# Attention over time and bands, then a feed-forward: the softmax weights become the stationary operand of the weighing, with a constant column beside the values

## The chip, the core and the metric

The kernel runs on one core of one Trainium2 chip. The time is device time in microseconds (us) of one execution of the whole program. The engines are TensorE (PE; its weight loads are listed apart as PEld), VectorE (DVE), ScalarE (ACT), GpSimd (POOL) and SyncE (SP), which issues most DMAs. Smaller is better.

## The reference

The input x has shape (2, 256, 128, 128): batch, time T, band FB, channel C. Three residual steps follow one another: causal attention along time, attention along bands within 16 bands of the query, and a feed-forward with 512 hidden channels. Everything is float32.

```python
def _mha(x, wi, bi, wo, bo, h, mask):
    qkv = x @ wi.T + bi
    q, k, v = jnp.split(qkv, 3, axis=-1)          # 4 heads of 32 channels
    scores = jnp.einsum('...hqd,...hkd->...hqk', q, k) * (1.0 / np.sqrt(dh)) + mask
    attn = jax.nn.softmax(scores, axis=-1)
    o = jnp.einsum('...hqk,...hkd->...hqd', attn, v)
    return o.swapaxes(-2, -3).reshape(x.shape) @ wo.T + bo

xt = _ln(x, ln_t_w, ln_t_b).transpose(0, 2, 1, 3)
x = x + _mha(xt, t_wi, t_bi, t_wo, t_bo, H_T, cm).transpose(0, 2, 1, 3)   # cm: causal, 256 steps
xf = _ln(x, ln_f_w, ln_f_b)
x = x + _mha(xf, f_wi, f_bi, f_wo, f_bo, H_F, bm)                          # bm: |i - j| <= 16
xn = _ln(x, ln_n_w, ln_n_b)
x = x + (gelu(xn @ w1.T + b1, approximate=False) @ w2.T + b2)
```

## The kernel before

A test on the device of how large the scores can become (`fold`) chooses between two paths; with these inputs the program takes `BoundedPath`, in which the exponential needs no row maximum. The other path isn't touched.

**Groups.** The work is cut into groups of 512 tokens: four tiles of 128 tokens. There are 128 groups of attention over time (`OverTime`: two bands of 256 steps each), 128 of attention over bands (`OverBands`: four time steps of 128 bands each) and 128 of feed-forward (`FeedForward`). All time groups come first; then eight band groups and the eight feed-forward groups that use them alternate. `run` is a software pipeline written out by hand: iteration n does one stage of each of several neighbouring groups, and every engine executes in exactly the order in which `run` emits (the wrapper `InOrder`). This is also why nearly all instructions in the profile carry the one line L924: it is the wrapper's.

**One attention group, stage by stage.** `normalize` and `turn` make the layer norm on DVE and transpose it in 32x32 blocks on DVE (the tile z), DMAs through DRAM (turned) finish the transpose, and `fetch` brings it back as xnT: channels on partitions, 512 tokens along the row. `queries_keys` and `values` multiply by the folded weights wf, and ACT copies the results out of PSUM as qT, kT and v. The scores go into PSUM with the keys on partitions and the queries along the row; ACT takes the exponential (tiles p; pf over bands), and POOL zeroes what the mask forbids. Over time the weights are in two tiles: p0 has the first 128 keys against all 256 queries, p1 the last 128 keys against the last 128 queries.

**Column tiles.** A product with 128 output rows is issued as four matmuls with 32 stationary columns each, one for each 32-column strip of the array, writing 32 partitions of PSUM each (`product`, `rows_of`). Such a matmul appears in the profile as "128*32" (rows * columns of the array). A float32 matmul of the program shows as two matmuls and two loads in the profile.

**The weighing (`weigh`, L758 over time, L845 over bands).** The stationary operand is v of one head (32 columns), and the softmax weights stream past as the moving operand, 128 to 256 queries at a time; the result op has channels on partitions and tokens along the row. A second set of matmuls with a stationary block of ones sums the weights into rp, in the same layout, each sum repeated on 32 partitions. Over time POOL first adds p1 to the part of p0 that belongs to the same queries (`add`, two calls), so that one pass of ones suffices.

**The division.** `invert` takes the logarithm of rp and the exponential of its negative on ACT (ln, then r). `divide` refines this by one Newton step on DVE (two operations, the second making u, with its sign reversed), and a third DVE operation multiplies op by u into oT. The reversed sign is taken up by wn, which is the output weight times -1. At the 16 places where band groups give way to feed-forward groups (`turn` in `run`), `invert_exactly` uses DVE's reciprocal instead, so that ACT needn't change its table.

**The output.** `output` multiplies oT by wn one iteration later, and `finish` adds the result to the residual on DVE.

**PSUM.** There are eight banks of 128x512. Over time their use is a fixed rotation (`banks`, `place`); over bands they are taken in turn (`turn_of_bank`).

**Order.** Iteration n over time emits for PE: scores of groups n and n+1, the output projection of group n-2, the weighing of n-1, queries and keys and then values of n+2. Over bands: scores of n, weighing of n-1, output projection of n-2, queries, keys and values of n+1. DVE's queue holds in each iteration the layer-norm work of groups three to eight ahead, the residual of n-2 and the division of n-1.

Of the kernel before, what the change touches and what calls it, by code (L numbers as in the profile page):

```python
# [19 lines left out]
P = 128  # L20
H = 4
# [10 lines left out]
BANK = 512  # L32
HALF = P // 2
LARGE = 1e20
EXP_SET = "natural_log_exp_and_others"


# [382 lines left out]
    return t.rearrange("p (t i q) -> p i t q", i=NT, q=D)  # L420


def by_tile(t):

    return t.rearrange("p (i t q) -> p i t q", i=NT, q=D)


class Group:
# [126 lines left out]
    def take_values(self):  # L555
        pass
# [1 line left out]
    def weigh(self):  # L558
        pass

    def invert(self):
        pass

    def divide(self):
        pass

# [25 lines left out]
class Attention(Group):  # L592
# [33 lines left out]
            product(path, self.vp[:, i], self.xnT[:, i * P : (i + 1) * P], wv, turn=2 if i in self.swapped else 0)  # L626

    def take_values(self):
        path = self.path
        self.v = path.work.tile([P, NT, P], F32, name="v", bufs=4)  # L630
        path.scalar.copy(self.v, self.vp)

    def invert(self):

        path = self.path
        ln = path.work.tile([P, NT * P], F32, name="ln", bufs=2)
        path.scalar.activation(ln, self.rp, AF.Ln)
        self.r0 = path.work.tile([P, NT * P], F32, name="r0", bufs=2)
        path.scalar.activation(self.r0, ln, AF.Exp, scale=-1.0)

    def invert_exactly(self):
        self.r0 = None
        self.r = self.path.work.tile([P, NT * P], F32, name="ln", bufs=2)
        self.path.vector.reciprocal(self.r, self.rp)

    def divide(self):

        path, vector = self.path, self.path.vector
        if self.r0 is None:
            self.oT = path.work.tile([P, NT * P], F32, name="oT", bufs=2)  # L650
            u = path.work.tile([P, NT * P], F32, name="u", bufs=2)
            vector.tensor_tensor(by_rows(u), by_tile(self.op), by_tile(self.r), ALU.mult)
            vector.tensor_scalar(self.oT, u, -1.0, None, ALU.mult)
            return
        vector.tensor_tensor(self.rp, self.rp, self.r0, ALU.mult)
        u = path.work.tile([P, NT * P], F32, name="u", bufs=2)
        vector.scalar_tensor_tensor(u, self.rp, 2.0, self.r0, ALU.subtract, ALU.mult)
        self.oT = path.work.tile([P, NT * P], F32, name="oT", bufs=2)
        vector.tensor_tensor(by_rows(self.oT), by_tile(self.op), by_tile(u), ALU.mult)

    def output(self):
        path = self.path
# [21 lines left out]
class OverTime(Attention):  # L684
# [15 lines left out]

    def take_values(self):
        path = self.path
        self.v = path.work.tile([P, NT, P], F32, name="v", bufs=4)
        for s in range(2):
            path.scalar.copy(self.v[:, 2 * s : 2 * s + 2], self.vp[s])

    def first_tiles(self):
        path = self.path
# [4 lines left out]
    def second_tiles(self):  # L713
        path = self.path

        self.p1 = path.work.tile([P, 2, H, 2, P], F32, name="p1", tag="h", bufs=2)
        self.s1 = {h: path.bank([P, 2, P], "sp", path.banks[f"b{h}"]) for h in range(H)}

    def first_scores(self, h, s, e):
# [16 lines left out]

    def second_weights(self, heads):
        for h in heads:
            self.path.scalar.activation(self.p1[:, :, h, 0], self.s1[h], AF.Exp)

    def mask(self, blk, base=0):
        path = self.path
# [6 lines left out]
        self.mask(self.p0[:, :, :, 0:P])  # L749

    def mask_second(self):
        self.mask(self.p1[0:HALF, :, :, 0], -HALF)
        self.mask(self.p1[HALF:P, :, :, 0, 0:HALF])

    def add(self, s):
        self.path.gpsimd.tensor_tensor(self.p1[:, s, :, 1], self.p1[:, s, :, 0], self.p0[:, s, :, P : 2 * P], ALU.add)

    def weigh(self):  # L758
        path, v = self.path, self.v
        rp = path.bank([P, 2, 2, P], "rp", self.place.get("rp"))  # L760
        for n in range(2):
            for h in range(H):
                w = self.p1[:, :, h, 1] if n else self.p0[:, :, h, 0:P]
                path.tensor.matmul(rp[rows_of(h), :, n], path.k.ones[:, 0:D], w, start=True, stop=True)
        op = path.bank([P, 2, 2 * P], "op", self.place.get("op"))
        for s in range(2):
            for h in range(H):
                r = rows_of(h)
                path.tensor.matmul(op[r, s, :], v[:, 2 * s, r], self.p0[:, s, h], start=True, stop=False)
            for h in range(H):  # L770
                r = rows_of(h)
                path.tensor.matmul(
                    op[r, s, P : 2 * P], v[:, 2 * s + 1, r], self.p1[:, s, h, 0], start=False, stop=True
                )
        self.op = op.rearrange("p s q -> p (s q)")
        self.rp = rp.rearrange("p s n q -> p (s n q)")


TIME_ORDER = """
# [19 lines left out]
class OverBands(Attention):  # L799
# [41 lines left out]
    def first_half(self):  # L841
        self.p = self.path.work.tile([P, H, NT, P], F32, name="pf", tag="p", bufs=3)
        self.scores(range(H))

    def weigh(self):  # L845
        path = self.path

        path.held = {name: path.turn_of_bank() for name in self.follow}
        self.rp = path.bank([P, NT * P], "rp")
        for h in range(H):  # L850
            path.tensor.matmul(
                self.rp[rows_of(h), :], path.k.ones[:, 0:D], self.p[:, h].rearrange("p i q -> p (i q)"),
                start=True, stop=True,
            )
        self.op = path.bank([P, NT * P], "op")
        for i in range(NT):
            c = slice(i * P, (i + 1) * P)
            for h in range(H):
                r = rows_of(h)
                path.tensor.matmul(self.op[r, c], self.v[:, i, r], self.p[:, h, i, :], start=True, stop=True)  # L860


class FeedForward(Group):
# [65 lines left out]
class BoundedPath:  # L929
    def __init__(self, ctx, tc, k):  # L930
        self.tc, self.nc, self.k = tc, tc.nc, k
        self.xpool = ctx.enter_context(tc.tile_pool(name="xpool", bufs=3))
        self.work = ctx.enter_context(tc.tile_pool(name="work", bufs=3))
        self.small = ctx.enter_context(tc.tile_pool(name="small", bufs=6))
        ps = ctx.enter_context(tc.tile_pool(name="ps", bufs=1, space=PSUM))
        self.ps = [ps.tile([P, BANK], F32, name=f"bank{i}", tag=f"bank{i}") for i in range(8)]
        self.next_bank = 0
        self.inputs = 0
        self.held = {}
        self.banks = dict(zip(("a1", "a2", "b0", "b3", "a0", "a3", "b1", "b2"), range(8)))  # L940
        self.tensor, self.vector = InOrder(tc, tc.nc.tensor), InOrder(tc, tc.nc.vector)
        self.scalar, self.gpsimd = InOrder(tc, tc.nc.scalar), InOrder(tc, tc.nc.gpsimd)
        self.sync = InOrder(tc, tc.nc.sync)
        self.dram = ctx.enter_context(tc.tile_pool(name="turns", bufs=3, space=DRAM))
        self.zero = 0.0
        self.once = once = ctx.enter_context(tc.tile_pool(name="once", bufs=1))
        self.eps = once.tile([P, 1], F32, name="eps")
        tc.nc.vector.memset(self.eps, EPS)

        self.band = once.tile([P, P], F32, name="band")  # L950
        tc.nc.gpsimd.memset(self.band, 0.0)
        for s in (1, -1):
            tc.nc.gpsimd.affine_select(
                out=self.band, in_=self.band, compare_op=ALU.is_ge, fill=-1e30, base=BAND,
                pattern=[[-s, P]], channel_multiplier=s,
            )

    def turn_of_bank(self):
        i, self.next_bank = self.next_bank, (self.next_bank + 1) % 8
# [109 lines left out]
    def fold_rest(self):  # L1069
# [32 lines left out]
    def warm(self):  # L1102


        for _ in range(8):
            bank = self.bank([P, 3 * P], "warm")
            self.tensor.matmul(bank, self.k.ones, self.k.wf[0], start=True, stop=True)

    def run(self, x, out):
        groups = list(self.groups(x, out))  # L1110
# [24 lines left out]
        for n in range(-12, len(groups) + 2):  # L1135
# [168 lines left out]
```

## Time and profile before

| | |
|---|---|
| median of 3 runs | 2663.48 us (2662.64 to 2663.9) |
| the profiled execution | 2662.95 us |
| its span in the trace | 2661.2 us |
| clock granted to TensorE | 0.999 |
| instructions in the trace | 156426 |
| DMA | 347.08 MB, mean 130 GB/s |

The groups of instructions that the change touches, from the groups by form (busy us is the time in which at least one of the group ran; matmuls on different column tiles run at once):

| engine, operation | shape | count | busy us | mean ns of one |
|---|---|---|---|---|
| PE sums over time, p with ones | 128x256 | 2048 | 134.0 | 379 |
| PE weighted values over time, p with v | 128x256 and 128x128 | 2048 and 2048 | 157.5 and 103.2 | 379 and 273 |
| PE sums over bands, pf with ones | 128x512 | 1024 | 140.6 | 603 |
| PE weighted values over bands, pf with v | 128x128 | 4096 | 140.7 | 273 |
| ACT ln and r | 128x512 | 240 each | 145.5 and 151.3 | 606 and 630 |
| DVE Newton step and product with op | 128x512 | 240 each of three | 166.9, 166.0, 166.0 | 695, 692, 692 |
| POOL adds of p | 128x512 | 256 | 323.9 | 1287 |

The span is cut into 40 slices on the page. The time groups fill roughly the first 14 of them, up to about 935 us; the rest alternates between bands and feed-forward. In a row of the timeline, the first number is the start and the second the time from the first start to the last end of the instructions merged in it.

### The profile page before, as it was taken

Reading aid. Unit: us, or ns where it says so; the run is one execution under the profiler, and the core shown is the slowest. Engines: PE = TensorE matmul, PEld = TensorE weight load, DVE = VectorE, ACT = ScalarE, POOL = GpSimd, SP = SyncE. Lnnn points to the kernel's source line nnn. Section 1 sums busy time; section 2 is a strip of 40 time slices with the busy share of each in tenths; the row PEclk is TensorE's granted clock in tenths of the full one; section 3 lists DMA queues with packets and bytes.
Section 4 is the critical chain, followed back from the end, with each engine's and each line's share of the span. In section 5 each row is a group of like instructions: output and inputs, shape, how many; then the busy total and the mean of one; then the engine's idle time right before and its main releaser. Section 6 shows DMA issues by size and latency. Waiting matters only on the chain.

```text
span 2661.2 us, 156426 instructions
## 1 busy us (share of the span) xinstructions
PE 2630.1 (99%) x68662; PEld 1930.4 (73%) x68662; DVE 2140.1 (80%) x6429; ACT 1841.8 (69%) x3562; POOL 1947.3 (73%) x2297
## 2 busy tenths in 40 slices
PE   7999999999999999999999999999999999999998
PEld 5667667666676668778777687777777877777777
DVE  6988888888888897977868779678687796886874
ACT  6898999989989874664755746647557466475573
POOL 4999999999999986756667667666676676666762
PEclk9999999999999999999999999999999999999999
DMA  6655555555556454444444444444444454544533
GB/s 147 159 155 149 152 153 153 150 151 157 149 154 153 121 129 120 124 122 126 118 118 126 122 118 126 120 125 118 123 125 119 117 129 113 133 118 121 127 95 82
DMA packets 471510, 347.08 MB, mean 130 GB/s; under 512 B 43296, under 2 KB 405152, under 8 KB 470816
## 3 DMA queue, kind: packets, MB, share of 16 engines
q1 hardware_dynamic: 469568, 335.92, 49.0%
q8 instruction: 540, 8.85, 1.5%
q10 hardware_dynamic: 1248, 1.05, 0.2%
q14 instruction: 154, 1.26, 0.2%
HBM read 169.03 MB, written 167.77 MB: 127 GB/s over the span
## 4 chain that ended last, share of the span: by engine, by line
PE 86%; DVE 10%; DMA 2%; SPq 0%; issue 0%; ACT 0%; DVEq 0%; ACTq 0%
PE bank L924 86%; DVE xh L924 2%; DVE bank L924 2%; DVE z L924 1%; DVE u L924 1%; DVE oT L924 1%; DVE stats L924 1%; DVE x L924 1%; DMA xnT<-turned 1%; DMA turned<-z 1%; SPq L924 0%; DVE mv L924 0%; DMA x<-in_x 0%; DMA rows_sb<-in_rows 0%; ACT p L924 0%
## 5 line engine op out<-in xcount | busy, mean ns | idle before, releaser
L924 ACT ACTIVATE hT<-bank,b 128x512 f32<-128x512 f32 x512 | 346.9, 688 | 527.0 <-PE bank L924 496.3
L924 POOL TENSOR_SCALAR_AFFINE_SELECT pf<-pf 128x512 f32<-128x512 f32 x768 | 476.8, 635 | 178.5 <-ACT pf L924 152.2
L924 PEld LDWEIGHTS bank<-w2T_sb,hT 128*32 128x32 f32 x16384 | 498.2, 110 | 22.9 <-issue 16.7
L924 PE MATMUL bank<-xnT,w1f 128*32 128x512 f32 x4096 | 510.0, 592 | 0.0
L924 PE MATMUL bank<-w2T_sb,hT 128*32 128x128 f32 x16384 | 504.0, 273 | 0.2 <-ACT hT L924 0.2
L924 PE MATMUL bank<-xnT,wf 128*32 128x512 f32 x4096 | 492.5, 592 | 3.5 <-ACT p L924 3.0
L924 ACT ACTIVATE p<-bank 128x512 f32<-128x512 f32 (+1 forms) x1024 | 430.4, 495 | 65.0 <-PE bank L924 64.6
L924 POOL TENSOR_SCALAR_AFFINE_SELECT p<-p 128x1024 f32<-128x1024 f32 (+2 forms) x384 | 363.6, 947 | 81.2 <-ACT p L924 72.9
L924 DVE TENSOR_SCALAR xh<-x,mv,rstd 128x160 f32<-128x160 f32 x1040 | 404.4, 431 | 9.7
L924 PEld LDWEIGHTS bank<-wf,xnT 128*32 128x32 f32 x8192 | 243.6, 110 | 144.0 <-issue 103.2
L924 DVE TENSOR_TENSOR res<-bank,res 128x512 f32<-128x512 f32 x256 | 170.5, 666 | 218.8 <-PE bank L924 192.0
L924 PEld LDWEIGHTS bank<-xnT,w1f 128*32 128x32 f32 x4096 | 247.2, 110 | 128.2 <-issue 114.9
L924 POOL TENSOR_TENSOR p<-p,p 128x512 f32<-128x512 f32 x256 | 323.9, 1287 | 10.7
L924 DVE BATCH_NORM_STATS2 stats<-x 128x6 f32<-128x128 f32 x1536 | 329.5, 277 | 0.2 <-DMA x<-in_x 0.2
L924 POOL TENSOR_SCALAR rstd<-mv 128x4 f32<-128x4 f32 x248 | 56.3, 227 | 369.1 <-DVE mv L924 368.3
L924 PE MATMUL bank<-qT,kT 32*64 32x80 f32 (+4 forms) x16384 | 314.3, 273 | 2.4 <-ACT p L924 1.0
L924 PEld LDWEIGHTS bank<-qT,kT 32*64 32x64 f32 x16384 | 271.3, 131 | 54.5 <-ACT kT L924 50.3
L924 ACT ACTIVATE pf<-bank 128x512 f32<-128x512 f32 x512 | 266.7, 602 | 46.7 <-PE bank L924 44.1
L924 PE MATMUL bank<-wn,oT 128*32 128x128 f32 x8192 | 283.4, 274 | 0.7 <-DVE oT L924 0.7
L924 DVE STREAM_TRANSPOSE z<-xh 128x512 f32<-128x512 f32 x384 | 273.3, 712 | 13.2
L924 PE MATMUL bank<-wf,xnT 128*32 128x128 f32 x8192 | 276.7, 273 | 0.0
L924 POOL TENSOR_TENSOR rstd<-rstd,mhalf 128x4 f32<-128x4 f32 x248 | 256.6, 1035 | 20.7
(102 smaller groups left out, 3806.0 us busy)
## 6 DMA issues: line engine op xcount, KB each, us to landing
turned<-z SPq DMA_DIRECT2D x1536, 64.0 KB, 2.7
xnT<-turned SPq DMA_DIRECT2D x384, 256.0 KB, 3.1
x<-in_x SPq DMA_DIRECT2D x128, 256.0 KB, 4.4
x<-res SPq DMA_DIRECT2D x256, 128.0 KB, 2.6
x<-x SPq DMA_DIRECT2D x128, 256.0 KB, 4.2
out<-res SPq DMA_DIRECT2D x256, 128.0 KB, 2.5
w1T_sb<-in_w1T ACTq DMA_DIRECT2D x1, 256.0 KB, 5.7
w2T_sb<-in_w2T ACTq DMA_DIRECT2D x1, 256.0 KB, 7.0
```

The lines of the kernel that those rows point to most:

```text
L924: return self.tc.keep_in_program_order(emit(*args, **kwargs))
```

## The change

The two operands of the weighing swap places. For each head, each 128-token tile and each block t of 32 queries, the 32 columns of softmax weights that belong to these queries are loaded as the stationary operand, and the head's values stream past: 32 channels and a 33rd column that holds a constant (UNIT, 2 to the power -10). The result has the queries on partitions, and beside the 32 weighted values stands the sum of the weights times UNIT. `terms` names which key tiles contribute: one, or two for the later 128 queries over time, which are accumulated in PSUM. So the passes with ones, the adds on POOL, the logarithm and exponential on ACT, the Newton step and the exact reciprocal at the turns are gone. `divide` does for each half (one bank) a DVE reciprocal of 8 sums per partition and a product of 256 values with them, broadcast over the channels, and then one transpose in 32x32 blocks into oT, with channels on partitions again. wn takes up UNIT.

The values live in four fixed tiles (`all_values`) whose constant column is set once by POOL; `next_values` hands them out in turn, and ACT's copy of v skips every 33rd column. p1 loses the room for POOL's sums. The warm-up matmuls at the start, eight in the program, read w1T (512 columns) instead of wf (384).

```diff
+UNIT = 2.0**-10
...
+def by_head(t):
+    return t.rearrange("p i (h d) -> p i h d", h=H)
...
     def take_values(self):
-        path = self.path
-        self.v = path.work.tile([P, NT, P], F32, name="v", bufs=4)
-        path.scalar.copy(self.v, self.vp)
-
-    def invert(self):
...
-    def invert_exactly(self):
...
+        self.v = self.path.next_values()
+        self.path.scalar.copy(self.v[:, :, :, 0:D], by_head(self.vp))
+
+    def weigh(self):
+        path = self.path
+        self.banks = [path.bank([P, 2 * NT, D + 1], name, self.place.get(name)) for name in ("rp", "op")]
+        for half, bank in enumerate(self.banks):
+            for t in range(NT):
+                for i in range(2):
+                    blk = bank[:, 2 * t + i]
+                    terms = self.terms(2 * half + i, t)
+                    for j, (keys, weights) in enumerate(terms):
+                        for h in range(H):
+                            path.tensor.matmul(
+                                blk[rows_of(h)], weights(h), self.v[:, keys, h],
+                                start=j == 0, stop=j == len(terms) - 1,
+                            )
 
     def divide(self):
 
         path, vector = self.path, self.path.vector
...
-        vector.tensor_tensor(self.rp, self.rp, self.r0, ALU.mult)
-        u = path.work.tile([P, NT * P], F32, name="u", bufs=2)
-        vector.scalar_tensor_tensor(u, self.rp, 2.0, self.r0, ALU.subtract, ALU.mult)
+        o = path.work.tile([P, NT, NT, D], F32, name="o", bufs=2)
+        for half, bank in enumerate(self.banks):
+            r = path.small.tile([P, 2 * NT], F32, name="r")
+            vector.reciprocal(r, bank[:, :, D])
+            vector.tensor_tensor(
+                o[:, :, 2 * half : 2 * half + 2].rearrange("p t i d -> p t (i d)"),
+                bank[:, :, 0:D].rearrange("p (t i) d -> p t i d", i=2), r.rearrange("p (t i) -> p t i", i=2).unsqueeze(3).to_broadcast([P, NT, 2, D]), ALU.mult,
+            )
         self.oT = path.work.tile([P, NT * P], F32, name="oT", bufs=2)
-        vector.tensor_tensor(by_rows(self.oT), by_tile(self.op), by_tile(u), ALU.mult)
+        vector.transpose(self.oT, o.rearrange("p t i d -> p (t i d)"))
...
 class OverTime(Attention):
...
+    def terms(self, i, t):
+        s, q = i // 2, slice(i % 2 * P + t * D, i % 2 * P + (t + 1) * D)
+        terms = [(2 * s, lambda h: self.p0[:, s, h, q])]
+        if i % 2:
+            terms.append((i, lambda h: self.p1[:, s, h, t * D : (t + 1) * D]))
+        return terms
...
-        self.p1 = path.work.tile([P, 2, H, 2, P], F32, name="p1", tag="h", bufs=2)
+        self.p1 = path.work.tile([P, 2, H, P], F32, name="p1", tag="h", bufs=2)
...
-    def add(self, s):
-        self.path.gpsimd.tensor_tensor(self.p1[:, s, :, 1], self.p1[:, s, :, 0], self.p0[:, s, :, P : 2 * P], ALU.add)
-
-    def weigh(self):
...
 class OverBands(Attention):
...
+    def terms(self, i, t):
+        return [(i, lambda h: self.p[:, h, i, t * D : (t + 1) * D])]
+
     def weigh(self):
-        path = self.path
-        path.held = {name: path.turn_of_bank() for name in self.follow}
-        self.rp = path.bank([P, NT * P], "rp")
...
+        self.path.held = {name: self.path.turn_of_bank() for name in self.follow}
+        super().weigh()
...
+        self.all_values = [once.tile([P, NT, H, D + 1], F32, name=f"v{i}") for i in range(4)]
+        for v in self.all_values:
+            tc.nc.gpsimd.memset(v[:, :, :, D], UNIT)
...
-            scalar.mul(wn, k.woT[a], -1.0)
+            scalar.mul(wn, k.woT[a], UNIT)
...
-            bank = self.bank([P, 3 * P], "warm")
-            self.tensor.matmul(bank, self.k.ones, self.k.wf[0], start=True, stop=True)
+            bank = self.bank([P, self.k.NI * P], "warm")
+            self.tensor.matmul(bank, self.k.ones, self.k.w1T, start=True, stop=True)
...
-                old.add(0)
-                old.add(1)
...
-            do(n - 1, "invert_exactly" if turn else "invert")
```

More of the change, by code (lines that the diff above doesn't have):

```diff
@@ L559, in weigh @@
         pass
-    def invert(self):
-        pass
     def divide(self):
@@ L628, in take_values @@
     def take_values(self):
+        self.v = self.path.next_values()
+        self.path.scalar.copy(self.v[:, :, :, 0:D], by_head(self.vp))
+    def weigh(self):
         path = self.path
-        self.v = path.work.tile([P, NT, P], F32, name="v", bufs=4)
-        path.scalar.copy(self.v, self.vp)
-    def invert(self):
-        path = self.path
[L636 to L639, printed above, removed]
@@ L641, in invert_exactly @@
-    def invert_exactly(self):
-        self.r0 = None
-        self.r = self.path.work.tile([P, NT * P], F32, name="ln", bufs=2)
-        self.path.vector.reciprocal(self.r, self.rp)
+        self.banks = [path.bank([P, 2 * NT, D + 1], name, self.place.get(name)) for name in ("rp", "op")]
[10 more added lines that the diff above has]
+                            )
@@ L646, in divide @@
     def divide(self):
         path, vector = self.path, self.path.vector
-        if self.r0 is None:
-            self.oT = path.work.tile([P, NT * P], F32, name="oT", bufs=2)
-            u = path.work.tile([P, NT * P], F32, name="u", bufs=2)
-            vector.tensor_tensor(by_rows(u), by_tile(self.op), by_tile(self.r), ALU.mult)
-            vector.tensor_scalar(self.oT, u, -1.0, None, ALU.mult)
-            return
-        vector.tensor_tensor(self.rp, self.rp, self.r0, ALU.mult)
-        u = path.work.tile([P, NT * P], F32, name="u", bufs=2)
@@ L702, in take_values @@
         path = self.path
-        self.v = path.work.tile([P, NT, P], F32, name="v", bufs=4)
+        self.v = path.next_values()
         for s in range(2):
-            path.scalar.copy(self.v[:, 2 * s : 2 * s + 2], self.vp[s])
+            path.scalar.copy(self.v[:, 2 * s : 2 * s + 2, :, 0:D], by_head(self.vp[s]))
+    def terms(self, i, t):
[4 more added lines that the diff above has]
+        return terms
     def first_tiles(self):
@@ L738, in second_weights @@
         for h in heads:
-            self.path.scalar.activation(self.p1[:, :, h, 0], self.s1[h], AF.Exp)
+            self.path.scalar.activation(self.p1[:, :, h], self.s1[h], AF.Exp)
     def mask(self, blk, base=0):
@@ L751, in mask_second @@
     def mask_second(self):
-        self.mask(self.p1[0:HALF, :, :, 0], -HALF)
-        self.mask(self.p1[HALF:P, :, :, 0, 0:HALF])
-    def add(self, s):
-        self.path.gpsimd.tensor_tensor(self.p1[:, s, :, 1], self.p1[:, s, :, 0], self.p0[:, s, :, P : 2 * P], ALU.add)
-    def weigh(self):
[L759 to L776, printed above, removed]
+        self.mask(self.p1[0:HALF], -HALF)
+        self.mask(self.p1[HALF:P, :, :, 0:HALF])
 TIME_ORDER = """
@@ L843, in first_half @@
         self.scores(range(H))
+    def terms(self, i, t):
+        return [(i, lambda h: self.p[:, h, i, t * D : (t + 1) * D])]
     def weigh(self):
-        path = self.path
-        path.held = {name: path.turn_of_bank() for name in self.follow}
-        self.rp = path.bank([P, NT * P], "rp")
[L850 to L860, printed above, removed]
+        self.path.held = {name: self.path.turn_of_bank() for name in self.follow}
+        super().weigh()
 class FeedForward(Group):
@@ L956, in __init__, with next_values @@
             )
+    def next_values(self):
+        self.all_values = self.all_values[1:] + self.all_values[:1]
+        return self.all_values[-1]
     def turn_of_bank(self):
```

## Prediction

> **What bounds the kernel now.** I read the page's busy row and its chain of waits first, to learn which engine sets the end.
>
> ```profile
> PE 2630.1 (99%) x68662; PEld 1930.4 (73%) x68662; DVE 2140.1 (80%) x6429; ACT 1841.8 (69%) x3562; POOL 1947.3 (73%) x2297
> PE 86%; DVE 10%; DMA 2%; SPq 0%; issue 0%; ACT 0%; DVEq 0%; ACTq 0%
> ```
>
> TensorE (PE) is without work for some 31 of 2661.2 us and makes up 86% of the chain that ended last. So time removed from PE can count, and time removed elsewhere counts only where PE would wait. Next I read PE's timeline over one steady group of the attention over time, then one of the attention over bands. Columns: start, length, then the instructions.
>
> ```profile
> 301.11 1.08 PE L924 MATMUL bank<-wn,oT 128*32 128x128 f32 x32
> 302.01 1.05 PE L924 MATMUL bank<-p,ones 128*32 128x256 f32 x16
> 302.87 1.48 PE L924 MATMUL bank<-p,v 128*32 128x256 f32 x32
> 304.17 1.90 PE L924 MATMUL bank<-xnT,wf 128*32 128x512 f32 x16
> ...
> 308.19 1.08 PE L924 MATMUL bank<-wn,oT 128*32 128x128 f32 x32
> ```
> ```profile
> 1703.75 1.06 PE L924 MATMUL bank<-qT,kT 32*64 32x80 f32 x64
> 1704.74 1.06 PE L924 MATMUL bank<-pf,ones 128*32 128x512 f32 x8
> 1705.63 1.06 PE L924 MATMUL bank<-pf,v 128*32 128x128 f32 x32
> 1706.50 1.06 PE L924 MATMUL bank<-wn,oT 128*32 128x128 f32 x32
> ...
> 1710.08 1.09 PE L924 MATMUL bank<-qT,kT 32*64 32x80 f32 x64
> ```
>
> Lengths overlap by the drain, so I subtract starts. One time group takes 308.19 - 301.11 = 7.08 us; its two weighing steps (the sums p,ones and the weighted values p,v) take 304.17 - 302.01 = 2.16. One band group takes 1710.08 - 1703.75 = 6.33; its weighing takes 1706.50 - 1704.74 = 1.76. There are 128 groups of each kind, so what the change touches is worth 128 x 3.92 = 502 us of PE. The same two stretches by engine (length, busy time with count in the order PE, PEld, DVE, ACT, POOL, then clock and DMA):
>
> ```profile
> 299.79:306.87 7.08, 7.08 (x196) 4.91 (x192) 5.89 (x18) 6.35 (x15) 6.55 (x7) 1.00 0.41 120
> 1703.75:1710.08 6.33, 6.33 (x189) 4.25 (x185) 5.97 (x12) 5.05 (x9) 3.98 (x7) 1.00 0.55 146
> ```
>
> The granted clock is full. Over time the next engines are POOL, 0.5 us below PE, and ACT; over bands it is DVE, only 0.36 below PE.
>
> **Change, first part: the matmuls of the weighing.** A program matmul shows as two in the profile (4 x 4 of the output projection show as 32). Over time the new weighing issues 2 halves x 4 t x (1 + 2 terms) x 4 heads = 96, so 192; over bands 64, so 128. Before it was 48 and 40. Each streams 33 columns instead of 128 to 512, but has its own load of 32 columns. By streaming alone, 32 matmuls of 128 columns take 302.01 - 301.11 = 0.90 us, 28 ns each with four column tiles side by side; 33 columns would be 28 x 33/128 = 7.2 ns. So the question is what one pair of load and short matmul costs when it isn't the stream that sets the pace. Break-even is 2.16/192 = 11.3 ns over time and 1.76/128 = 13.8 ns over bands.
>
> No such stream is in the trace. The nearest is the scores over bands, 64 pairs with 80 columns, and the start of the sums behind them:
>
> ```profile
> 963.39 0.97 PE L924 MATMUL bank<-qT,kT 32*64 32x80 f32 x64
> 963.39 0.81 PEld L924 LDWEIGHTS bank<-qT,kT 32*64 32x64 f32 x64 [0.20 <-ACT kT L924]
> 964.29 0.16 PEld L924 LDWEIGHTS bank<-pf,ones 128*32 128x32 f32 x8
> 963.39:963.71 0.32, 0.32 (x36) 0.32 (x33) 0.32 (x1) 0.18 (x1) 0.32 (x1) 1.00 0.28 74
> ```
>
> The last load of 64 starts 0.81 - 0.13 (one load) = 0.68 us after the first: 10.6 ns each. The first 33 fall into 0.32 us: 9.7 ns. The eight loads of exactly the new form (128 rows, 32 columns) start within 0.16 - 0.11 = 0.05 us: 7 ns, though each lasts 110, so loads for different column tiles do run side by side. Lower bound: 7 ns. Upper bound: all 64 score matmuls with the drain behind them, 1704.74 - 1703.75 = 0.99 us, 15.5 ns each. I take 9.7, since the scores' loads are twice as wide and their streams longer, while eight loads are too few to show what a run of 192 sustains. The second half of those 64 is slower (31 in 0.36 us, 11.6 ns), which keeps the upper end alive.
>
> Over time: 192 x 9.7 = 1.86, so -0.30 us a group, x 128 = -38 us. ACT loses ln and r (0.593 + 0.630 = 1.22 us), POOL two adds of 1.287, so neither becomes a bound. Over bands: 128 x 9.7 = 1.24, so -0.52 on PE; here DVE comes in.
>
> [...]
>
> **Second part: divide on DVE.** Gone are three passes of 128x512 at 692 ns (groups by form: bank<-bank,r; u<-bank,r; oT<-bank,u), 2.08 us. New, per half: a reciprocal of 128x8 and a product of 128x256, then one transpose. The transpose is known: z<-xh 128x512, 712 ns. The product is not in the trace: 128x128 takes 292 and 128x512 takes 692, 1.04 ns an element more; 256 elements take 425. The reciprocal of 128x512 takes 3319, so 8 elements 52 ns, plus the 144 that a 4-element operation takes: 0.20. Sum 2 x 0.625 + 0.712 = 1.96; bounds 2 x (0.144 + 0.345) + 0.712 = 1.69 (with the 128x256 scalar form of 345) and 2 x (0.22 + 0.53) + 0.712 = 2.21 (171 for a 16-element operation plus 52; the 431 of a 160-element xh plus 96 x 1.04). So DVE changes by -0.12 (-0.39 to +0.13) a group; over time it stays a microsecond below PE. Over bands it goes from 5.97 to 5.85 against PE's 6.33 - 0.52 = 5.81: both are then the bound. With the small waits that remain I take 6.0 us, -0.33 x 128 = -42 us instead of -67. Before a group's divide, DVE now waits for PE's first half alone; its queue holds the statistics behind it, with a whole iteration of slack before PE's output projection needs oT.
>
> **Third part: the turns.** Where bands give way to the feed-forward, DVE did an exact reciprocal:
>
> ```profile
> L924 DVE RECIPROCAL ln<-bank 128x512 f32<-128x512 f32 x16 | 53.1, 3319 | 0.0
> PE bank L924 <- DVE oT L924: 4.3, 13, 0.7
> ```
>
> It takes 53 us on DVE, but PE waited only 4.3 us for oT in all; feed-forward groups are PE's and DVE has room there (36.5 of 56.4 us from 1118.60 on). I count -4.
>
> **The rest.** The warm-up's 16 matmuls grow from 384 to 512 columns: 7.53 x 512/384 = 10.0 us, and the first projection follows at once, so +2.5. Four memsets, the scale of wn and the strided copy of v (same 128x256 and 128x512 sizes) cost nothing: ACT and POOL, with 1.2 and 2.6 us freed per group over time, hide them; without that cover it would be 0.1 us each, once, for the memsets. No DMA is added or moved.
>
> Sum: -38 - 42 - 4 + 2.5 = -81.5 against the profiled span of 2661.2, which is 2580; the median stands 2.3 us above that span, so 2582.
>
> **Rivals.**
> *The pair is slow (slower).* Beyond the first 33 pairs the rate falls, and a run of 192 lives off that. From 11.3 ns over time it loses there, and from about 12.3 ns overall (502 us / 40960 matmuls). At 15.5: (2.98 - 2.16) x 128 = +105 and (1.98 - 1.76) x 128 = +28, 2796 with the small terms. For it: the 11.6 of the second half. Against: these loads are half as wide. Chance 0.17.
> *Loads serialize per tile (slower).* If the next matmul on a tile must wait for a 110 ns load, four tiles give 27.5 ns: (5.28 - 2.16 + 3.52 - 1.76) x 128 = +625, 3287. Against it: eight loads in 0.16 us. Chance 0.06.
> *Gain swallowed.* At 11.3 ns, or if DVE (2.21 a divide) holds bands at 6.2: time +0 and bands -0.13 to -0.3, that is -17 to -38: 2625 to 2645. Chance 0.13, of which 0.03 within no change.
> *Streaming bounds it.* At 7.2 ns: (2.16 - 1.38) x 128 = -100, bands at DVE's 5.85, -61: about 2501. Chance 0.09.
> The forecast has 0.55.
>
> **Numbers.** About 0.2% is what a measurement of this kernel can tell from no change. Faster is 0.55 + 0.09 + 0.10 = 0.74, same 0.03, slower 0.23. The range of 8 in 10 runs from the streaming case to a pair of 13 ns: 2505 to 2695. The likeliest case alone, 9 to 10.6 ns, runs from 2560 to 2605.
>
> **What would show it.** PE's timeline: 192 matmuls of 33 columns in 1.9 us between the output projection and xnT,wf, 128 in 1.24 over bands, and group periods of 6.8 and 6.0. DVE busy near 97% over bands. The prediction is wrong if the pair takes over 11.3 ns, if PE then waits for DVE's r or oT, or if idle time of PE put down to "issue" appears inside the short matmuls.

## The result, and the profile after

The changed kernel takes 3383.48 us (median of 4 runs, 3367.32 to 3397.81) against 2663.1 before: a ratio of 1.270, 95% interval 1.264 to 1.276. It is 720 us slower, where 81 us less was predicted, and lies far outside the range.

The profile of the changed kernel, at a span of 3396.0 us: busy row, chain of waits, the DMA row of the instructions, and PE's longest wait.

```profile
PE 2786.1 (82%) x98358; PEld 2060.7 (61%) x98358; DVE 2091.2 (62%) x6941; ACT 1588.6 (47%) x3082; POOL 1632.6 (48%) x2045
PE 82%; issue 17%; ACT 0%; DMA 0%; DVE 0%; DVEq 0%; ACTq 0%
q8 instruction: 773, 12.66, 1.6%
PE bank L901 <- issue: 574.1, 379, 3.8
```

PE fell from 99% busy to 82%, and no other engine took its place: all are busy for a smaller share of the span than before. 17% of the chain, which was 0%, is "issue": time in which PE waited for nothing that the profile can name. These waits add up to 574.1 us in 379 stops (0.6 us before), out of 735 us between the two spans. The groups by form put it into the weighing above all (last column: idle time before the group, and what ended it):

```profile
L901 PE MATMUL bank<-v,p 128*32 128x33 f32 x24576 | 290.5, 201 | 307.6 <-issue 303.1 <-ACT p L901 4.1
L901 PE MATMUL bank<-v,pf 128*32 128x33 f32 x16384 | 208.1, 201 | 125.1 <-issue 125.0
```

PE's timeline over a little more than one group over time. It is the counterpart of the rows from 301.11 on in the kernel before.

```profile
303.94 1.08 PE L901 MATMUL bank<-wn,oT 128*32 128x128 f32 x32
304.84 0.36 PE L901 MATMUL bank<-v,p 128*32 128x33 f32 x22
305.86 1.32 PE L901 MATMUL bank<-v,p 128*32 128x33 f32 x128 [0.66 <-issue]
309.62 0.58 PE L901 MATMUL bank<-v,p 128*32 128x33 f32 x42 [2.44 <-issue]
310.05 3.25 PE L901 MATMUL bank<-xnT,wf 128*32 128x512 f32 x16
...
315.78 1.08 PE L901 MATMUL bank<-wn,oT 128*32 128x128 f32 x32
```

The 192 short matmuls come as 22, then a stop, then 128, a longer stop, then 42. The middle part is 128 matmuls with 128 loads: 256 instructions. That is one packet of the row q8, which has 16 KB (12.66 MB in 773 packets): PE's 196716 matmuls and loads by 773 packets are 254 each, and before the change 137324 by 540 were also 254. I call the 256 instructions of a packet a page. The middle part runs in 1.32 - 0.20 = 1.12 us (0.20 is the length of the last one), so a pair cost 8.7 ns here once it was there. Then PE stands still. From the first stop's end to the second's it is 309.62 - 305.86 = 3.76 us for one page. This group took 11.84 us instead of 7.08.

The trace has the times of the single packets too. Two of q8 landed at 304.45 and 308.08, and the two stops of the rows above ended at 305.86 and 309.62, 1.4 and 1.5 us later. It is the same over the whole run: of the 400 gaps of over 20 ns in PE's matmuls after the first 50 us, nine in ten ended 1.2 to 1.6 us after a packet of q8 had landed. With a packet every 4.1 us, one in ten would do so by chance.

How the loss divides between the stages shows in the first start of the loads for the weighted values over bands, before and after:

```profile
L924 PEld LDWEIGHTS bank<-pf,v x4096: 106/110/110, 952.3 to 2597.7; 128*32 128x32 f32 x196
```
```profile
L901 PEld LDWEIGHTS bank<-v,pf x16384: 106/109/162, 1439.6 to 3330.9; 128*32 128x32 f32 x200
```

The time groups end 487 us later; the other 248 of the 735 us between the two spans are lost between there and the end. One stretch of the time stage, before and after, in the table by engine (second number: length; then busy time and count of PE and PEld):

```profile
300.00:899.00 599.00, 599.00 (x16264) 416.00 (x16256) 508.78 (x1503) 540.22 (x1227) 554.05 (x509) 1.00 0.58 152
```
```profile
300.00:899.00 599.00, 446.70 (x18736) 325.52 (x18728) 333.83 (x1103) 298.26 (x700) 225.34 (x223) 0.91 0.38 101
```

Before, PE was busy throughout and went through 32520 instructions, one page of 256 in 4.72 us. After, it went through 37464, one page in 4.09 us, and idled for a quarter of the time. So the theory to test was: PE's program arrives in pages of 256 instructions, at best one in 3.5 to 4 us (an estimate from the 3.76 and 4.09 us above), and the new weighing has more instructions than that supply.

### The profile page after: what moved, and what is told of

Read it like the earlier page. It is cut to its first block, busy times and chain, and to the rows that moved or that the text cites. A ratio compares the mean times of both kernels' runs of the same rounds, so it can differ in the third digit from the quotient of the medians.

```text
span 3396.0 us, 215827 instructions
## 1 busy us (share of the span) xinstructions
PE 2786.1 (82%) x98358; PEld 2060.7 (61%) x98358; DVE 2091.2 (62%) x6941; ACT 1588.6 (47%) x3082; POOL 1632.6 (48%) x2045
## 3 DMA queue, kind: packets, MB, share of 16 engines
q8 instruction: 773, 12.66, 1.6%
## 4 chain that ended last, share of the span: by engine, by line
PE 82%; issue 17%; ACT 0%; DMA 0%; DVE 0%; DVEq 0%; ACTq 0%
PE bank L901 81%; ACT p L901 0%; DMA f_wiT_sb<-in_f_wiT 0%; DMA xnT<-turned 0%; PE gq L901 0%; ACT kT L901 0%; DMA turned<-z 0%; DVE xh L901 0%; PE gk L901 0%; DVE z L901 0%; PE brp L901 0%; ACT lnv L901 0%; DVE stats L901 0%; DVE tests L901 0%; ACT hT L901 0%
## 5 line engine op out<-in xcount | busy, mean ns | idle before, releaser
L901 PE MATMUL bank<-xnT,wf 128*32 128x512 f32 x4096 | 631.6, 706 | 47.4 <-issue 42.8
L901 ACT ACTIVATE qT<-bank,bq 128x512 f32<-128x512 f32 x256 | 176.1, 688 | 858.8 <-PE bank L901 858.8
L901 PE MATMUL bank<-v,p 128*32 128x33 f32 x24576 | 290.5, 201 | 307.6 <-issue 303.1
L901 PEld LDWEIGHTS bank<-w2T_sb,hT 128*32 128x32 f32 x16384 | 480.1, 110 | 45.0 <-issue 24.6
L901 PEld LDWEIGHTS bank<-v,p 128*32 128x32 f32 x24576 | 267.2, 112 | 329.0 <-issue 325.0
L901 PEld LDWEIGHTS bank<-wf,xnT 128*32 128x32 f32 x8192 | 297.8, 118 | 204.5 <-issue 150.0
L901 PE MATMUL bank<-wn,oT 128*32 128x128 f32 x8192 | 311.1, 284 | 71.1 <-issue 67.4
L901 PE MATMUL bank<-wf,xnT 128*32 128x128 f32 x8192 | 339.1, 288 | 28.9 <-issue 27.5
L901 PEld LDWEIGHTS bank<-xnT,wf 128*32 128x32 f32 x4096 | 172.9, 124 | 250.9 <-issue 228.6
L901 DVE RECIPROCAL r<-bank 128x8 f32<-128x8 f32 x512 | 103.1, 201 | 348.5 <-PE bank L901 340.6
```

The lines of the kernel that those rows point to most:

```text
L901: return self.tc.keep_in_program_order(emit(*args, **kwargs))
```

## The experiments

**e1: the old weighing with as many instructions.** The kernel before, with matmuls cut over their columns. The pieces of queries and keys take the four strips in turn; in the sums and in p0 with v the pieces of one head follow one another on one strip.

```diff
-        product(path, self.qp, wf[:, 0:P], self.xnT)
+        product(path, self.qp, wf[:, 0:P], self.xnT, parts=4)
...
             for h in range(H):
                 r = rows_of(h)
-                path.tensor.matmul(op[r, s, :], v[:, 2 * s, r], self.p0[:, s, h], start=True, stop=False)
+                for e in range(4):
+                    q = slice(e * HALF, (e + 1) * HALF)
+                    path.tensor.matmul(op[r, s, q], v[:, 2 * s, r], self.p0[:, s, h, q], start=e < 3, stop=e < 2)
```

> The kernel before, whose weighing is left as it was, with its matmuls cut into narrower ones over the same columns (queries and keys 512 -> 4x128; sums and weighted values into pieces of 64 or 128), so that a time group has 336 matmuls and a band group 272 in the profile, exactly as many as after the change. Same streaming time, same DVE, ACT and POOL. Theory (code supply): PE's instructions arrive in pages of 256, one page each 3.9 us, so a time group of 672 instructions takes 10.2 to 10.9 us whatever they are, and the total is 3200 to 3400 us. Rival (the 33-column matmuls and their loads are slow in themselves): the total stays under 2700 us.

Measured: 3324.03 us, ratio 1.249 (1.245 to 1.252). No matmul has 33 columns here, no softmax weight is stationary, DVE, ACT and POOL do what they did before, and the loss is 662 us. But it is not the same loss. PE's timeline over the weighing and the products behind it, and PE's wait by the profile:

```profile
403.37 2.50 PE L938 MATMUL bank<-p,ones 128*32 128x64 f32 x61
405.85 2.54 PE L938 MATMUL bank<-p,v 128*32 128x64 f32 x76
408.14 0.28 PE L938 MATMUL bank<-xnT,wf 128*32 128x128 f32 x3
408.25 1.89 PE L938 MATMUL bank<-xnT,wf 128*32 128x128 f32 x60
409.89 0.29 PE L938 MATMUL bank<-wf,xnT 128*32 128x128 f32 x3
PE bank L938 <- issue: 87.3, 153, 1.8
```

The queries and keys, in 64 pieces with the strips in turn, take 409.89 - 408.14 = 1.75 us, as the 16 wide matmuls did (1.72). The weighing takes 408.14 - 403.37 = 4.77 instead of 2.16 us, at an even pace with one stop of some 0.1 us. The width of the pieces isn't it: over bands the sums are cut into pieces of 128 columns, like the queries and keys, but one strip at a time, and take 1.87 us instead of 0.88 in the median group. So in e1 the pieces that follow one another on one strip ran side by side only in part: the 64 of the sums over time took 2.3 us, 36 ns each, and the 64 of the queries and keys, twice as wide and with the strips in turn, 27. Over all groups the weighing takes 4.6 us in the median over time and 3.0 instead of 1.76 over bands: some 470 of the 662 us, a loss of the edit's own. Stops put down to "issue" are 87.3 us. In the stretch from 300 to 899 us PE went through

```profile
300.00:899.00 599.00, 576.61 (x19383) 543.68 (x19378) 354.63 (x1027) 375.68 (x836) 377.26 (x346) 1.00 0.40 106
```

38761 instructions, one page in 3.96 us, about the pace of the changed kernel (4.09), so the supply may have been close to its limit as well. But e1 can't part the two: that its total lies in the range of the theory is in good part chance, and the rival, that short matmuls are slow in themselves, has to fall by the timeline above and by the runs below.

**e2 and e3: one part alone.** The new weighing over time only, or over bands only (`TimeSwapped` is the changed code's `weigh` and `divide` as a subclass of the old class).

```diff
-                    yield OverTime(self, partial(part, "x", g), ...
+                    yield (TimeSwapped if time_swapped(n_time) else OverTime)(self, partial(part, "x", g), ...
```

> New weighing over time alone, old weighing over bands. Code supply: the time groups cost what they cost after the change, 10.9 us instead of 7.08, so +487 us: about 3150 us; the band groups go back to 6.3 us. Rival (a shared cause such as the lower granted clock or a queue that fills over the whole program): not additive, off from 3150 by more than 60 us.

> New weighing over bands alone, old weighing over time. Code supply: a run of 8 band and 8 feed-forward groups takes 119.9 us instead of 106.6, so +213 us: about 2876 us. Rival (bands gain and only the time stage loses): below 2663 us.

Measured: 3135.18 us (ratio 1.178, 1.174 to 1.181) and 2902.63 us (1.090, 1.087 to 1.093) against 2662.37. The losses, 473 and 240, add up to 713 of 720: each stage loses for itself, and bands don't gain either. Expected were 3150, met within 15 us, and 2876, exceeded by 27.

**e4: fewer instructions beside an unchanged weighing.**

```diff
-    for c in range(P // D):
-        path.tensor.matmul(out[rows_of(c)], weights[:, rows_of((c + turn) % NT)], x, start=start, stop=stop)
+    if turn == 0:
+        path.tensor.matmul(out, weights, x, start=start, stop=stop)
+        return
...
```

> The changed kernel, weighing untouched, but each product of 128 output rows is one matmul with 128 stationary columns instead of four with 32 (two of 64 for the two tiles whose halves are swapped over time). The columns streamed stay the same; a time group falls from 336 to 280 matmuls, a band group from 272 to 212, a feed-forward group from 160 to 40. Code supply: a time group takes 560/256 x 3.9 = 8.5 us, a band group 424/256 x 3.9 = 6.5 or less: total 2780 to 2950 us. Rival (short matmuls slow in themselves): stays near 3380 us, since the weighing is the same.

Measured: 3147.13 us, ratio 1.182 (1.179 to 1.186). The weighing is the same and 236 us came back, so the loss is not the weighing's own; but it is some 200 us above the range that the mean supply gave. PE's timeline shows a reason:

```profile
408.66 1.69 PE L906 MATMUL bank<-v,p 128*32 128x33 f32 x172
412.73 0.38 PE L906 MATMUL bank<-v,p 128*32 128x33 f32 x20 [2.38 <-issue]
413.05 1.99 PE L906 MATMUL bank<-xnT,wf 128*128 128x512 f32 x4
414.87 1.54 PE L906 MATMUL bank<-wf,xnT 128*128 128x128 f32 x12
...
418.74 1.47 PE L906 MATMUL bank<-v,p 128*32 128x33 f32 x146
421.92 0.61 PE L906 MATMUL bank<-v,p 128*32 128x33 f32 x46 [1.70 <-issue]
```

The long matmuls of 413.05 to 416.34 now take only 32 instructions, so there are 418.74 - 413.05 = 5.7 us in which instructions could arrive; yet the next burst of 384 instructions, from 418.74 on, stops after 146 of its 192 matmuls. So no more than these 292 instructions were at hand, with what came meanwhile. The mean over a group was not enough here: the supply would have had to hold over each burst. Another part of the missing 200 us may lie in the edit itself (e6).

**e5: without the turn's DMAs.** The second half of each transpose is left out.

```diff
-        z = path.work.tile([P, H, P], F32, name="z", bufs=2)
+        self.xnT = path.work.tile([P, NT * P], F32, name="xnT")
         path.vector.transpose(
-            z.rearrange("p c (t q) -> p c t q", q=D), self.xh
+            self.xnT.rearrange("p (c t q) -> p c t q", c=H, q=D), self.xh
         )
...
-            path.sync.dma_start(self.turned[:, :, i, :].rearrange("c a x -> a c x"), z[rows_of(i)])
...
```

> The changed kernel without the DMAs of the turn: DVE's 32x32 blocks go straight into xnT, so the second half of each transpose is left out (1536 writes and 384 reads, about 200 of the 336 MB of data). PE's program stays the same. Theory (a page of 256 PE instructions costs a fixed 3.5 to 4 us of fetch, one after the other): the page interval stays at 3.4 us or more at its shortest and the total within 2% of 3383 us. Rival (the page waits for the data DMAs on the same DMA engines): the shortest intervals fall below 3 us and the total below 3100 us.

Measured: 3355.4 us, 0.8% below the change. In the same stretch the DMA engines are busy 0.22 instead of 0.38 of the time, and PE gets hardly more:

```profile
300.00:899.00 599.00, 448.26 (x18946) 325.51 (x18941) 338.72 (x1120) 301.05 (x707) 227.93 (x224) 0.93 0.22 53
```

37887 instructions, one page in 4.05 us against 4.09. Nearly half of the traffic less changed a page by 1%: the data traffic was not the main thing that a page waited for here.

**e6, e7, e8: can pages ahead carry a part of the change?** e6 is the edit of e4 on the kernel before; e7 uses the new weighing in every fourth group of each attention, e8 in every second one (`n % 2 == 1`) together with e6. In e7:

```diff
+def time_swapped(n):
+    return n % 4 == 3
...
+def bands_swapped(n):
+    return n % 4 == 3
```

> The kernel before with each product of 128 output rows as one matmul with 128 stationary columns (the edit of e4 alone). Code falls from 384 to 272 instructions a time group, 368 to 248 a band group, 320 to 80 a feed-forward group. Theory A (changing between 128- and 32-column loads lets the array run empty, about 0.2 us each, two more a time group and one more a band group): about 2740 us. Theory B (no such cost, and the kernel before was free of fetch waits): 2663 us within 0.5%. If the kernel before already lost to code supply, it gets faster than 2650.

> The new weighing in every fourth group of each attention (the last of four), the old one in the others; products as before. Code supply as a mean: (3 x 384 + 672)/4 = 456 instructions a time group in some 7 us, 65 a us, just what a page in 3.9 us gives; if the pages fetched ahead carry the group of 672, each new group gains 0.5 us: about 2625 us. Rival (only about two pages are fetched ahead, so a group of 672 is starved wherever it stands): each new time group loses some 2 to 3 us, total 2720 to 2800 us.

> Every second group with the new weighing, products with 128 stationary columns as in e6. Mean code: (560 + 272)/2 = 416 instructions a time group, (424 + 248)/2 = 336 a band group, so 6.3 and 5.1 us of fetch: under PE's own time. If pages fetched ahead carry over a group: 60 us under e6. Rival (starved locally): 64 x 2 us over time and 64 x 0.3 over bands lost, 100 to 150 us over e6.

Measured: e6 2809.71 us (ratio 1.054, 1.051 to 1.057), e7 2837.14 (1.065, 1.062 to 1.068), e8 2931.58 (1.100, 1.097 to 1.103). e6 lost twice what theory A gave: fewer instructions, 145 us more. Its changes of tile shape were the reason for expecting a loss, and its trace fits them: in a time group around 407 us the starts of two matmuls lie some 0.11 us apart within the output projection and 0.20 where its shape gives way to the next (407.33, 407.44, 407.64). The twelve matmuls of the values, with four changes, take 1.47 us instead of 0.98. No run takes the changes away alone, so that they are the whole cause is only argued. In e7 the mean supply would do, and 172 us were lost: the rival holds, a group of 672 instructions is starved wherever it stands, and the total lies above even the rival's 2800 us. e8 lies 122 us over e6, as its rival said.

**e9: the supply by itself.** PE alone; matmuls of 33 and of 512 columns on four column tiles, and the layer is left out. One run.

```diff
+    run(8, 512)
+    run(512, 33)
+    for _ in range(6):
+        run(24, 512)
+        run(128, 33)
...
```

> PE alone, without any other DMA while it works: 2048 program matmuls of 33 columns on four column tiles in one stretch (8192 instructions, 32 pages), then six times a stretch of long matmuls (384 instructions at about 107 ns a matmul) followed by a burst of 2048 instructions. The layer itself is left out and the output is one constant block. Theory (fixed time per page): the long stretch takes 32 x 3.4 to 3.9 us = 109 to 125 us, and each burst runs at 8.3 ns a matmul (1.06 us a page) for as many pages as were fetched ahead, one or two, and then stops at every page. Rival (the page time comes from the load on the DMA engines): below 2.5 us a page without that load. Rival (fetched far ahead): the first four pages or more of a burst without a stop.

Measured, three rows of the long stretch of short matmuls, then two behind a long stretch of wide ones:

```profile
26.40 1.99 PE L22 MATMUL bank<-w 128*32 128x33 f32 x128 [1.47 <-issue]
29.86 1.99 PE L22 MATMUL bank<-w 128*32 128x33 f32 x128 [1.47 <-issue]
33.31 1.99 PE L22 MATMUL bank<-w 128*32 128x33 f32 x128 [1.47 <-issue]
...
145.38 2.49 PE L22 MATMUL bank<-w 128*32 128x512 f32 x227
149.94 1.81 PE L22 MATMUL bank<-w 128*32 128x33 f32 x128 [2.07 <-issue]
```

With next to no other DMA at work (the DMA engines are busy 0.02 of the stretch) the stops come after every 128 matmuls, 256 instructions, and a page takes 3.45 us (29.86 - 26.40, 33.31 - 29.86), and some in the long stretch 3.7 to 4.0. At 3.45 that is 13.5 ns an instruction, 27 ns a pair, where a pair took a third of it, 8.7 ns, in the changed kernel at a granted clock of 1.00. The row at 145.38 merges the last 4 wide matmuls with the burst behind them: after some 20 us of wide matmuls, with time for five pages, 223 short ones ran until the next stop, 446 instructions. In three of the six bursts it was 223, in the other three 159:

```profile
386.27 1.96 PE L22 MATMUL bank<-w 128*32 128x512 f32 x163
```

At 256 a page, 446 and 318 instructions are the rest of the page in use and one more. So one page or a little over was at hand in these bursts, never four. Most of the page time, 3.45 us, is there with the DMA engines busy 0.02 of the time; what makes the 4.05 to 4.09 us of the kernels out of it isn't shown.

**e10: the only place that seemed to have pages to spare.** As e7, with bands `n % 8 == 7` and no time group.

> The new weighing only in the last band group of each run of eight, whose weighing follows the 64 instructions of the first feed-forward group's long matmuls; every other group as before. In e7 and in the changed kernel the weighing of just these groups took 1.4 to 1.6 us against 1.76 before. Code supply: pages are ready there, so each of the 16 places gains 0.2 to 0.4 us, and DVE is spared the exact reciprocal: 2650 to 2660 us. Rival (a group of more code delays the ones behind it): 2663 or more.

Measured over 8 runs: 2673.0 us, ratio 1.0035 (1.0024 to 1.0045). Slower by 9 us: the rival. PE's wait by the profile, 0.6 us before, and two of the sixteen places:

```profile
PE bank L1007 <- issue: 9.6, 14, 1.4
1103.64 1.77 PE L1007 MATMUL bank<-v,pf 128*32 128x33 f32 x126
...
1531.88 1.30 PE L1007 MATMUL bank<-v,pf 128*32 128x33 f32 x95
1534.58 0.47 PE L1007 MATMUL bank<-v,pf 128*32 128x33 f32 x33 [1.40 <-issue]
```

Without a stop the weighing takes 1105.22 - 1103.64 = 1.6 us, a little under the old 1.76; with one, 2.98. The gains are smaller than the losses even here. No version was found that beats the kernel before.

**e11: half of the new weighing.** Two of the four query blocks are left out.

```diff
-            for t in range(NT):
+            for t in range(NT // 2):
```

> The changed kernel with two of the four query blocks t left out of the weighing (the values of the other half are whatever the bank held); all else as after the change. A time group has 240 matmuls, 480 instructions, a band group 208 and 416. Code supply: 480/256 x 3.9 = 7.3 us a time group and 6.3 a band group, little above the 7.08 and 6.33 of before, so most of the loss is gone with half of the added work: 2690 to 2800 us (the upper end if a burst of 192 runs past the two pages that are at hand). Rival (each short matmul costs the same wherever it stands): half of the matmuls, half of the loss: about 3020 us less the work saved, 2900 or more.

Measured: 2784.76 us, ratio 1.044 (1.041 to 1.047). That is in the theory's range, and there are stops here too:

```profile
309.14 0.79 PE L901 MATMUL bank<-v,p 128*32 128x33 f32 x66
312.75 0.61 PE L901 MATMUL bank<-v,p 128*32 128x33 f32 x27 [2.82 <-issue]
```

But the rival's 2900 us left out that the old weighing, 502 us of PE, is gone in both kernels. An even price per short matmul would be (720 + 502)/40960 = 29.8 ns by the change, and half of them would cost 20480 x 29.8 ns - 502 = 109 us more than before; measured are 118 (against 2667.04). So e11 doesn't part the two, and neither do e2, e3 and e7, which an even price meets within 25 us. What excludes it is the same weighing beside other work. With the products of e4 and e6 in both kernels, the new weighing costs 3147.13 - 2809.71 = 337 us and not 720; half of the groups (e8 less e6) cost 122 and not some 360; the 16 groups of e10 cost 9 and not 33.

## Why the prediction was wrong

**The step that failed** is the term "what one pair of load and short matmul costs", where it is applied to a run of 192: 192 x 9.7 = 1.86 us. The price was not the error. With its instructions at hand a pair took 8.7 ns, better than the 9.7 taken, and loads of 110 ns on the four column tiles did run side by side: 128 pairs in 1.12 us here, and in the kernel before the 32 pairs of the output projection in 0.90. The error is that PE's queue was taken to be full: instructions were counted to be multiplied by an execution time, and never as something that has to arrive. By pages, the time group is 672/256 = 2.6 pages; at e9's 3.45 us that is 9.1 us, at the 4.09 of the changed kernel's time stage 10.7, where before it took 7.08. It measured some 10.9 (7.08 + 487/128): 3.8 us more a group, where 0.30 less was forecast. The band group is 544/256 = 2.1 pages, 7.3 us at 3.45, instead of 6.33; it lost 248/128 = 1.9 us, where 0.33 less was forecast. The feed-forward groups win none of it back (6.93 us each before and after).

The rows for this were in the profile of before: 540 instruction packets of 16 KB in 2661 us, nearly all of them PE's (137324/256 = 536), one in 4.9 us, for an engine whose count was to grow by 43% (68662 to 98358 pairs). They had no price, since nothing was starved then, and e9 is what gives it. The scores, from which the price of a pair was taken, are 64 pairs, 128 instructions: half a page, too short to show it. The slower second half of those 64 was read as a property of the pair; what made it slower wasn't looked into.

**Point by point.** The 192 matmuls in 1.9 us between the output projection and xnT,wf: wrong, 310.05 - 304.84 = 5.2 us in the group shown, with the "issue" inside the short matmuls that the prediction named as a sign against itself. DVE's new divide was right; the form groups after the change give 201 ns for the reciprocal (0.20 predicted), 425 for the product (425) and 712 for the transpose:

```profile
L901 DVE TENSOR_TENSOR o<-bank,r 128x256 f32<-128x256 f32 x512 | 217.4, 425 | 17.6
L901 DVE RECIPROCAL r<-bank 128x8 f32<-128x8 f32 x512 | 103.1, 201 | 348.5 <-PE bank L901 340.6
```

But DVE as the bound over bands never came up: over both stages it waited for PE for 340.6 us before the reciprocals alone. The turns' 4 us can't be seen beside the loss, though PE's waits no longer have a row for oT. The warm-up grew from 7.5 to 8.7 us, half of the 2.5 allowed. The rival "loads serialize per tile" had a total near the measured one, 3287, and a wrong cause: 128 pairs in 1.12 us exclude 27.5 ns a pair. That the totals agree is chance. "The pair is slow" is wrong for the pair and right in its sign; its point of decision, 11.3 ns, was indeed passed by the 13.5 ns x 2 at which instructions arrive.

What is left of the 735 us beside the 574 of stops is not settled. A part goes with the lower granted clock, 0.946 over the run against 0.999 before. The same 16 long matmuls behind the weighing, before and behind the stop at 309.62:

```profile
304.17:305.89 1.72, 1.72 (x25) 0.52 (x21) 1.39 (x2) 1.72 (x4) 1.64 (x3) 1.00 0.55 143
310.05:313.00 2.95, 2.95 (x30) 0.94 (x24) 2.62 (x13) 0.69 (x1) 0.00 (x0) 0.58 0.09 26
```

They take 2.95 us instead of 1.72 at a granted clock of 0.58 instead of 1.00. No run takes the stops or the clock away alone.

## What to carry to other kernels

Count PE's instructions per microsecond, and not only the work in them: a matmul of float32 was four here (two loads, two matmuls), and more than 256 in 3.5 to 4 us starved PE in these runs, wherever the stretch was longer than the page or two at hand. The smaller tiles of the new weighing, which raise that count, lost time in every run that had them (473 us in e2, 240 in e3, 172 in e7, 9 in e10). Idle PE time put down to "issue", in stops that come 128 matmuls apart, was its sign in these profiles (574.1 us in 379 stops), and the times of the instruction packets confirmed it. A cheap test before a rewrite is to cut the same streams into more pieces; in e1 the cut cost some 470 us of its own where the pieces didn't take the strips in turn. And a test against an even price per instruction has to count what the change took away: e11 looked like a proof only without the old weighing's 502 us.

## What the runs showed of the hardware that was not expected

The instructions of PE came in pages of 256, each 3.45 us at the shortest spacing of e9's rows, with next to no other traffic, and 4.05 to 4.09 us on average in e5 and the changed kernel, with the DMA engines busy 0.22 and 0.38 of the time. In the changed kernel PE went on 1.2 to 1.6 us after a page had landed, in nine of ten gaps. In e9 the stops came after every 128 matmuls, 256 instructions, and 446 or 318 instructions ran until the first stop behind some 20 us of wide matmuls. In the changed kernel these stops are the 17% of the chain that is "issue".

Pieces on one strip, one behind the other, ran side by side only in part: in e1 the 64 matmuls of 64 columns for the sums took 2.3 us, where in the kernel before 16 of 256 columns had taken 0.86 with the strips in turn.

In the changed kernel and in e9 the stops went with a lower granted clock (third number from the end). In e9's stretch of short matmuls, with a stop in each page, it was 0.50; in the next one, of wide matmuls for the most part, 0.94:

```profile
22.95:116.95 94.00, 53.35 (x3453) 49.87 (x3456) 0.00 (x0) 0.00 (x0) 0.50 0.02 5
124.00:145.50 21.50, 21.50 (x210) 6.00 (x204) 0.00 (x0) 0.00 (x0) 0.94 0.01 2
```

At 0.50, 128 short matmuls took some 1.8 us instead of the 1.1 in the changed kernel at 1.00, with stops of 1.5 to 2 us between them. That the stops lower the clock is the author's reading and isn't shown by a run of its own: e1, with 153 stops of 0.6 us in the mean (87.3 us), was granted 0.999.
